# Second stage's edges: halves of the first batch in swapped parts, mask maxima one in three slots, last two turns interleaved

## The chip, the cores and the metric

The kernel runs on one core of a Trainium2 chip, alone on it. The metric is the device time of one execution in microseconds (us), the median of several runs. The core has five instruction streams: TensorE (PE, matrix products; its weight loads are listed as PEld), VectorE (DVE), ScalarE (ACT), GpSimd (POOL) and SyncE (SP, which here issues nearly all DMA transfers). Each stream runs its own instructions in order[...]. [...]

## The reference, cut to what matters

Input `x` is 128 graphs (batches) of 128 nodes with 128 features, `adj` an integer matrix 128 x 128 for each batch. Four graph layers follow one another, each as `x = x + layer(relu(layernorm(x)))`. The second of them is the one that this change touches:

```python
D = |x[:, :, None, :] - x[:, None, :, :]|          # (B, 128, 128, 128): all pairs of nodes
h = D @ W1.T + b1                                  # 64 features a pair
h = batchnorm(h; mean and variance over all pairs of all batches)
h = where(h >= 0, h, 0.01 * h)
s = h @ W2.T + b2                                  # one score a pair
s = where(A > 0, s, -9e15)                         # A: the adjacency
A = softmax(s)
y = (A @ x) @ Wg.T + bg
y = batchnorm(y; over all nodes of all batches)
y = where(y >= 0, y, 0.01 * y)
out = concat([x, y]) @ Wt.T + bt
```

The two batch norms take their statistics over everything, so nothing after the first can start before the last pair is in, and nothing after the second before the last `y` is there. They cut the kernel into three stages.

## The kernel before

**Stage one** (up to about 1455 us) computes the first graph layer and, for every batch, the products of `W1` with the pair differences. Symmetry halves the pairs: a batch needs the offsets 1 to 64 between two nodes, in two sets of 32, which stand on the two halves of the 128 partitions (64 features each). That gives `z`, 128 partitions x 4096 values a batch, kept as two **halves** of 128 x 2048 f32 (1 MB each). Of 124 batches they are written to HBM (`HP[b]`); those of the last four stay on chip. After that come the statistics of the first batch norm: `scale1`, `bias1`.

**Stage two** (to 2244 us) runs the 128 batches in **slots**, from -1 up to 140. The first four are those that stayed on chip; the others are read back from HBM by `fetch`. A ring of ten half-batch buffers holds them (`ahead_by` = 10): in slot `b`, SP issues the fetches of the halves `2 * b + 10` and `2 * b + 11` (L662), and each of them waits until its buffer in the ring, that of the half ten earlier, has been read for the last time. A slot does, for three batches at once:

- batch `b + 1`, preparation. The two halves go two different ways to the same function. The one called `z0` is scaled and shifted in place by ACT (L850) and made leaky by DVE, max of 0.01 z and z (L868). The one called `z1` is left as it is; ACT writes its scaled Relu to `zr` (L854).
- batch `b`, products. PE forms the scores in a bank `ps` (three of them), four matmuls for each part, 512 columns each: `w2z` with `z0`; then `w2l` with the raw `z1` (0.01 of scale and weight: the linear part) and `w2r` with `zr` (0.99 of the weight). A constant that the raw part lacks is put back by `add_k`, whose columns 4 to 7 belong to the half that went the second way and 0 to 3 to the other.
- batch `b - 1`, rearranging. DVE copies `ps` to `su` (L846), PE turns it with `pick` (L832, function `by_k`), DVE adds `add_k` and writes it to `sk` (L839, L841, function `to_sk`).

Four batches make a **turn**. A turn's function `chain` puts its steps into named places of coming slots with `at(slot, place, work)`; `slot` runs the places "am", "e", "p", "a", "l", "s" between its own instructions. So the order on every engine is written out by hand, and it is the order in which the engines run. In a turn, `to_rows` writes `sk` to HBM with a skewed address pattern and reads that turn's `x` (L902, L905); `from_rows` reads the scores back as `u` with rows and columns in place (L909); `normed` makes the layer norm on DVE (L244, L255), with the mask cap and `x + bt` on POOL (L914, L916); `folded` and `scores` add `u`, its transpose and the cap (L920, L924, L925); then maximum, exponential (L970, ACT), sums, weights, and products on PE with a copy to SBUF by ACT after each (L889, L894, L898, L948, L952). `stored` takes the statistics of `y` (L955). The turns' small PE results take three banks "sm" in rotation. Turn 31 is the last; the places of its steps are counted from `s0`, as are all.

In the slots 12 to 37 a side job, `brief`, works out whether a bound holds that lets stage three run without row maxima. It also looks for the largest value in the adjacency masks: `highest(g)`, one reduce over a mask of 128 x 512 bytes (L1045) for each of 32 groups, and `decided` at its end.

**Stage three** (430 us) needs the statistics of all `y` (L1116); its order comes from a planner and starts from the five groups that stayed on chip.

Of the kernel before, what the change touches and what calls it, by code (L numbers as in the profile page):

```python
# [13 lines left out]
AF = mybir.ActivationFunctionType  # L14
# [3 lines left out]
P = 128  # L18
G = 4
# [150 lines left out]
def tile_gnn_stack(ctx: ExitStack, tc: tile.TileContext, a: dict, out: bass.AP):  # L170
    nc = tc.nc
    NB = a["x"].shape[0]
    NG = NB // G
# [93 lines left out]
    def two_stages(general):  # L267
# [504 lines left out]
        with tc.tile_pool(name="c1", bufs=1, reuse_waits="tile") as c1, \  # L772
# [26 lines left out]

            sk = []  # L800
# [20 lines left out]
            def products(ps, parts, j0):  # L821
                for i, (w, v) in enumerate(parts):
                    for c in range(4):
                        w0 = 31 - 2 * (j0 // 4)
                        nc.tensor.matmul(ps[32 * c:32 * c + 32, :], w[:, w0:w0 + 32], v[:, 512 * c:512 * c + 512],  # L825
                                         start=j0 == 0, stop=w is w2r, skip_group_check=True)
# [8 lines left out]
            def to_sk(b):  # L835

                s, k, pk = sk[b // G % 2], b % G, scored.pop(b)[1]
                out_k = s[:, k, 1:].rearrange("p (a b) -> p b a", b=4)
                nc.vector.tensor_tensor(out_k, pk[:, :, 0:16], add_k.rearrange("p h j -> p (h j)")[:, None, :]  # L839
                                        .to_broadcast([P, 4, 16]), OP.add)  # L840
                nc.vector.tensor_scalar(s[:, k, 2 * KH:], s[:, k, 2 * KH:], 0.5, None, op0=OP.mult)  # L841

            def slot(b):
                if b - 1 in scored:
                    su = p1.tile([P, 4, P], F32, name="su")
                    nc.vector.tensor_copy(su.rearrange("p a b -> p (a b)"), scored[b - 1])  # L846
                    scored[b - 1] = su, sm("pk", "pk")
                if b + 1 < NB:
                    z0, z1 = fetched.pop(0), fetched.pop(0)
                    nc.scalar.activation(z0, z0, AF.Identity, bias=bias1, scale=scale1[:, 0:1])  # L850
                now(b, "am")
                if b + 1 < NB:
                    zr = p1.tile([P, NT // 2 * KC * P], F32, name="zr", bufs=3)
                    nc.scalar.activation(zr, z1, AF.Relu, bias=bias1, scale=scale1[:, 0:1])  # L854
                    prepared[b + 1] = z0, z1, zr
                now(b, "e")
                if b in prepared:
                    z0b, z1b, zrb = prepared.pop(b)
                    ps = psum.tile([P, 512], F32, tag="ps", bufs=banks["ps"], name="ps")
                    products(ps, [(w2z, z0b)], 0)  # L860
                    products(ps, [(w2l, z1b)], 4)
                if b - 1 in scored:
                    by_k(b - 1)
                if 0 <= b < NB:
                    products(ps, [(w2r, zrb)], 4)
                    scored[b] = ps
# [4 lines left out]
                if b - 1 in scored:  # L871
                    to_sk(b - 1)
                now(b, "l")
# [5 lines left out]
            def chain(turn):  # L879
# [5 lines left out]
                s0 = G * turn + 2 * G + 1 - 2 * final  # L885
# [14 lines left out]
                def to_rows():  # L900
                    to = rows[0, 0, 0:1]
                    nc.sync.dma_start(bass.AP(tensor=to.tensor, offset=to.offset,  # L902
                                              ap=[[ROW + 1, P], [P * ROW, G], [1, 1 + 2 * KH]]), own_sk)
                    t["x"] = p1.tile([P, G, P], F32, name="x", bufs=3)
# [33 lines left out]
                def weights():  # L938
                    nc.vector.tensor_tensor(t["e"], t["e"], t["sums"][:, :, None].to_broadcast([P, G, P]), OP.mult)
                    nc.vector.tensor_tensor(t["x1"], t["x1"], t["po"], OP.add)  # L940

                def product(name, left, right):
                    t[name] = sm(name)
                    four(t[name], left, right)
# [15 lines left out]
                at(G * turn + G + 1 - final, "s", to_rows)  # L960
                at(G * turn + G + 3 - 2 * final, "s", from_rows)
                at(s0, "e", normed)
                at(s0, "p", lambda: turned("pt", t["h"]))
                at(s0, "l", folded)
                at(s0 + 1, "am", lambda: copied("hT", "pt"))
                at(s0 + 1, "p", lambda: turned("put", t["u"]))
                at(s0 + 1, "l", scores)
                at(s0 + 2, "e", less_max)
                at(s0 + 2, "p", lambda: product("po", lambda k: t["hT"][:, k, :], lambda k: wtxT))
                at(s0 + 2, "a", lambda: nc.scalar.activation(t["e"], t["e"], AF.Exp))  # L970
                at(s0 + 2, "l", summed)
                at(s0 + 3, "e", weights)
                at(s0 + 3, "p", lambda: turned("pa", t["e"]))
                at(s0 + 3, "a", lambda: copied("aT", "pa"))
                at(s0 + 4, "p", lambda: product("py", lambda k: t["h"][:, k, :], lambda k: t["aT"][:, k, :]))
                at(s0 + 5, "am", lambda: copied("yT", "py"))
                at(s0 + 5, "p", last_product)
                at(s0 + 6, "am", biased)
                at(s0 + 7, "e", stored)
# [13 lines left out]
            def brief():  # L993
                t, end = {}, 3 * G
                searched = end + 9 + NG // 2
# [104 lines left out]
                for g in range(NG):  # L1100
                    at(end + 9 + g // 2, "l", lambda g=g: highest(g))
# [532 lines left out]
```

## Time and profile before

| | us |
|---|---|
| median of 3 runs | 2674.77 (2673.55 to 2675.49) |
| the profiled execution | 2676.09 |
| its span, first to last instruction | 2674.20 |
| DVE busy | 2469.6 (92% of the span) |
| PE busy | 2437.0 (91%) |
| ACT busy | 2380.3 (89%) |
| POOL busy | 1706.1 (64%) |
| first ACT pass of stage two | 1459.35 |
| first fetch of stage two issued | 1465.81 |
| last fetch of stage two issued | 2185.1 |
| aggregate of the statistics of `y` | 2244.33 |
| mean TensorE clock granted, share of full | 0.98 |

A line of the profile's order in time has the start in us, the duration in us, the engine, the line of the kernel (L...), the operation, the tiles written and read with their shapes, and how many; in brackets, how long the engine stood idle before it and what it waited for. A group line has the number of instructions, busy time in us, mean in ns, and the idle time before them. "issue" is time in which an engine waited for nothing that the profile shows. The DMA row of the page gives in tenths how full the 16 DMA engines are.

### The profile page before, as it was taken

What the parts mean: (1) busy time and instruction counts of PE and PEld (TensorE: products, weight loads), DVE (VectorE), ACT (ScalarE), POOL (GpSimd) and SP (SyncE); (2) the same over time, 40 slices, a digit from 0 to 9 for tenths busy, and PEclk for the clock granted to TensorE, in tenths of its full rate; (3) what the DMA queues carried; (4) which work ended last, traced back from release to release, by engine and by line L of the source; (5) the groups of instructions that cost most, each with busy time, mean ns of one, the idle gap of its engine ahead of it and who ended that gap; (6) DMA issues with size and microseconds to landing.
All of it is one profiled execution on the core that took longest, in us unless ns stands there. A gap on an engine that the chain in (4) does not pass through costs nothing.

```text
span 2674.2 us, 41925 instructions
## 1 busy us (share of the span) xinstructions
PE 2437.0 (91%) x14521; PEld 1162.1 (43%) x14521; DVE 2469.6 (92%) x4738; ACT 2380.3 (89%) x2821; POOL 1706.1 (64%) x1628
## 2 busy tenths in 40 slices
PE   6999999999999999999997988888888886999997
PEld 3333333333333333333332443444444445777776
DVE  5999999999999999999998789988888886899997
ACT  5999999999999999999998877788778874999997
POOL 6999999999999999999985000010101123666663
PEclk8999999999999999999998999999999998999999
DMA  3555555555555555555542999999999992021211
GB/s 101 201 206 209 212 212 211 212 213 205 209 205 209 205 210 204 217 204 216 205 197 93 409 409 384 392 409 410 411 410 411 410 373 81 21 68 56 64 37 34
DMA packets 185426, 611.43 MB, mean 229 GB/s; under 512 B 31987, under 2 KB 99702, under 8 KB 121718
## 3 DMA queue, kind: packets, MB, share of 16 engines
q1 hardware_dynamic: 184768, 608.50, 59.1%
q8 instruction: 118, 1.93, 0.3%
q14 instruction: 102, 0.84, 0.1%
q10 hardware_dynamic: 438, 0.17, 0.0%
HBM read 312.58 MB, written 296.03 MB: 228 GB/s over the span
## 4 chain that ended last, share of the span: by engine, by line
PE 37%; ACT 24%; DVE 15%; DMA 12%; POOL 7%; issue 4%; SPq 0%; POOLq 0%; DVEq 0%; ACTq 0%
PE hp L338 16%; ACT d L376 9%; ACT z L352 7%; DMA z<-hp 4%; PE hp L341 4%; DMA rows<-sk 4%; PE ps L825 4%; POOL d L328 4%; DMA u<-rows 3%; DVE z L868 3%; ACT o L473 2%; PE pk L832 2%; ACT hn L473 2%; PE xp L414 1%; DVE e L1502 1%
## 5 line engine op out<-in xcount | busy, mean ns | idle before, releaser
L328 POOL TENSOR_TENSOR d<-xe 128x2048 f32<-128x2048 f32 x256 | 1073.8, 4205 | 36.4 <-PE hp L338 34.5
L338 PE MATMUL hp<-d,w1T 128*64 128x512 f32 x4096 | 994.1, 601 | 57.6 <-ACT z L352 54.5
L376 ACT ACTIVATE d<-d 128x2048 f32<-128x2048 f32 x384 | 733.8, 1924 | 19.8 <-POOL d L328 19.5
L328 DVE TENSOR_TENSOR d<-xe,xp 128x2048 f32<-128x2048 f32 x256 | 583.6, 2280 | 7.0 <-POOL xe L423 4.0
L352 ACT COPY z<-hp 128x1024 f32<-128x1024 f32 x512 | 519.1, 1015 | 9.7 <-PE hp L338 4.5
L338 PEld LDWEIGHTS hp<-d,w1T 128*64 128x64 f32 x4096 | 276.9, 136 | 559.5 <-issue 455.3
L916 POOL TENSOR_TENSOR x<-x,bt 128x512 f32<-128x512 f32 x32 | 48.8, 1525 | 665.7 <-DMA x<-x 494.1
L366 DVE BATCH_NORM_STATS2 st<-z 128x6 f32<-128x512 f32 x512 | 354.7, 693 | 6.2 <-ACT z L352 6.1
L367 DVE BATCH_NORM_STATS2 st<-z 128x6 f32<-128x512 f32 (+1 forms) x512 | 336.4, 657 | 0.0
L868 DVE SCALAR_TENSOR_TENSOR z<-z 128x2048 f32<-128x2048 f32 x128 | 299.5, 2340 | 5.5 <-ACT z L850 5.3
L850 ACT ACTIVATE z<-z,bias,scale 128x2048 f32<-128x2048 f32 x128 | 267.5, 2090 | 8.9 <-DVE bias L762 7.7
L854 ACT ACTIVATE zr<-z,bias,scale 128x2048 f32<-128x2048 f32 x128 | 267.7, 2092 | 0.5 <-DMA z<-hp 0.5
L341 PE MATMUL hp<-both_t,xw 128*64 128x512 f32 x1024 | 265.2, 592 | 0.0
L825 PE MATMUL ps<-z,w2z 128*32 128x512 f32 x1024 | 140.9, 622 | 61.2 <-DVE z L868 60.5
L832 PEld LDWEIGHTS pk<-pick,su 128*128 128x128 f32 x1024 | 126.8, 195 | 147.8 <-DVE su L846 112.9
L832 PE MATMUL pk<-pick,su 128*128 128x16 f32 x1024 | 139.4, 268 | 34.6 <-DVE su L846 33.8
L825 PE MATMUL ps<-zr,w2r 128*32 128x512 f32 x1024 | 142.5, 629 | 0.0
L341 PEld LDWEIGHTS hp<-both_t,xw 128*64 128x64 f32 x1024 | 77.6, 137 | 142.2 <-issue 142.2
L825 PE MATMUL ps<-z,w2l 128*32 128x512 f32 x1024 | 138.4, 610 | 0.0
L1525 PE MATMUL pv<-wr,e 128*128 128x128 f32 x1024 | 134.0, 278 | 2.1 <-ACT wr L1450 1.1
L1525 PEld LDWEIGHTS pv<-wr,e 128*128 128x128 f32 x1024 | 124.1, 192 | 8.4 <-ACT wr L1450 1.8
L1409 ACT ACTIVATE h<-x,nb,rs 128x128 f32<-128x128 f32 x256 | 106.0, 491 | 20.1 <-POOL nb L1404 18.4
(241 smaller groups left out, 3808.3 us busy)
## 6 DMA issues: line engine op xcount, KB each, us to landing
hp<-z SPq DMA_DIRECT2D x248, 1024.0 KB, 4.0
z<-hp SPq DMA_DIRECT2D x248, 1024.0 KB, 13.7
x<-x SPq DMA_DIRECT2D x118, 256.0 KB, 4.8
u<-rows SPq DMA_DIRECT2D x32, 384.0 KB, 11.4
x<-in_x_dram SPq DMA_DIRECT2D x32, 256.0 KB, 5.6
adj<-in_adj_dram SPq DMA_DIRECT2D x32, 256.0 KB, 5.9
out_dram<-x SPq DMA_DIRECT2D x32, 256.0 KB, 2.4
z<-y SPq DMA_DIRECT2D x27, 256.0 KB, 11.8
```

Of the source, the lines that this page charges most:

```text
L328: eng.tensor_tensor(d, ahead, x[:, None, None, :].to_broadcast([P, 2, KC, P]), OP.max if t == BY_MAX else OP.subtract)
L338: nc.tensor.matmul(hp[64 * hh:64 * hh + 64, c:c + 512], w1T2 if by_max else w1T, d[:, hh, c:c + 512], start=True, stop=not by_max, skip_gr ...
L341: nc.tensor.matmul(hp[64 * hh:64 * hh + 64, c:c + 512], XW[i // NT // 2][:, i // NT % 2, :], both_t.rearrange("p h k i -> p h (k i)")[:, h ...
L352: nc.scalar.copy(half_of(b, t), linear.pop(i))
L366: nc.vector.bn_stats(st[:, 2 * t, :], hs[:, 0:512])
L367: nc.vector.bn_stats(st[:, 2 * t + 1, :], hs[:, 512:1024 - P * last])
L376: nc.scalar.activation(diffs[i], diffs[i], AF.Abs)
L825: nc.tensor.matmul(ps[32 * c:32 * c + 32, :], w[:, w0:w0 + 32], v[:, 512 * c:512 * c + 512], start=j0 == 0, stop=w is w2r, skip_group_chec ...
L832: nc.tensor.matmul(pk[:, kk, 0:16], su[:, kk, :], pick.rearrange("p h j -> p (h j)"), start=True, stop=True)
L850: nc.scalar.activation(z0, z0, AF.Identity, bias=bias1, scale=scale1[:, 0:1])
L854: nc.scalar.activation(zr, z1, AF.Relu, bias=bias1, scale=scale1[:, 0:1])
L868: nc.vector.scalar_tensor_tensor(z0, z0, 0.01, z0, op0=OP.mult, op1=OP.max)
```

## The change

Three parts.

- First batch: `z0` and `z1` change places in slot -1, and ACT makes the Relu before the linear pass. In slot 0, PE takes the raw part first, then the Relu part, then `w2z`. As the columns of the scores change with the places, a second constant tile, `add_0` (sixteen columns of the scratch tile `selfb`), holds `add_k` with its two parts swapped.
- Mask maxima: `highest(g)` goes to slot `end + 9 + 3 * g` with `end` = 12: 32 reduces in the slots 21, 24, ... 114; before, two in each of the slots 21 to 36. `decided` moves to slot 118.
- Last two turns: turns 30 and 31 get plans of their own, and a new place "k", just behind `to_sk`. The read of `x` becomes a function of its own, `again`. Turn 30 starts up to three slots earlier (its read-back `u` at slot 126, not 127; norm 126, not 129), and its value product goes to a bank "ps". Turn 31 asks for its `x` at slot 125, before its rows; its rows go out in slot 128 as before. The steps of both turns alternate. `joined` is split off `weights`. Turn 29 moves one ACT step by part of a slot.

```diff
+            add_0 = selfb[:, G - 1, P - 16:].rearrange("p (h j) -> p h j", h=2)
+            nc.vector.tensor_copy(add_0[:, :, 4:8], add_k[:, :, 0:4])
+            nc.vector.tensor_copy(add_0[:, :, 0:4], add_k[:, :, 4:8])
...
-            def products(ps, parts, j0):
-                for i, (w, v) in enumerate(parts):
-                    for c in range(4):
-                        w0 = 31 - 2 * (j0 // 4)
-                        nc.tensor.matmul(ps[32 * c:32 * c + 32, :], w[:, w0:w0 + 32], v[:, 512 * c:512 * c + 512],
-                                         start=j0 == 0, stop=w is w2r, skip_group_check=True)
+            def products(ps, w, v, j0, start=False, stop=False):
+                for c in range(4):
+                    w0 = 31 - 2 * (j0 // 4)
+                    nc.tensor.matmul(ps[32 * c:32 * c + 32, :], w[:, w0:w0 + 32], v[:, 512 * c:512 * c + 512],
+                                     start=start, stop=stop, skip_group_check=True)
...
-                nc.vector.tensor_tensor(out_k, pk[:, :, 0:16], add_k.rearrange("p h j -> p (h j)")[:, None, :]
+                nc.vector.tensor_tensor(out_k, pk[:, :, 0:16], (add_k if b else add_0).rearrange("p h j -> p (h j)")[:, None, :]
...
+                linear = lambda z: nc.scalar.activation(z, z, AF.Identity, bias=bias1, scale=scale1[:, 0:1])
+                first = b + 1 == 0
                 if b + 1 < NB:
                     z0, z1 = fetched.pop(0), fetched.pop(0)
-                    nc.scalar.activation(z0, z0, AF.Identity, bias=bias1, scale=scale1[:, 0:1])
+                    if first:
+                        z0, z1 = z1, z0
+                    else:
+                        linear(z0)
                 now(b, "am")
                 if b + 1 < NB:
                     zr = p1.tile([P, NT // 2 * KC * P], F32, name="zr", bufs=3)
                     nc.scalar.activation(zr, z1, AF.Relu, bias=bias1, scale=scale1[:, 0:1])
+                    if first:
+                        linear(z0)
...
-                    products(ps, [(w2z, z0b)], 0)
-                    products(ps, [(w2l, z1b)], 4)
+                    if b:
+                        products(ps, w2z, z0b, 0, start=True)
+                    products(ps, w2l, z1b, 4 * (b > 0), start=b == 0)
                 if b - 1 in scored:
                     by_k(b - 1)
                 if 0 <= b < NB:
-                    products(ps, [(w2r, zrb)], 4)
+                    products(ps, w2r, zrb, 4 * (b > 0), stop=b > 0)
+                    if b == 0:
+                        products(ps, w2z, z0b, 4, stop=True)
...
                 if b - 1 in scored:
                     to_sk(b - 1)
+                now(b, "k")
                 now(b, "l")
...
-                s0 = G * turn + 2 * G + 1 - 2 * final
+                s0 = G * turn + 2 * G + 1
...
+                if last < 2:
+                    at(s1, "s", to_rows)
+                    at(s1, "s", again)
+                    at(s1 + 2 - last, "s", from_rows)
+                else:
+                    at(s1 - 4, "s", again)
+                    at(s1 - 1, "s", to_rows)
+                    at(s1, "s", from_rows)
...
+                elif last == 1:
+                    plan = ((-3, "k", normed), (-2, "p", lambda: turned("pt", t["h"])), (-2, "k", folded),
+                            (-2, "l", lambda: turned("put", t["u"])), (-1, "am", lambda: copied("hT", "pt")),
+                            (-1, "k", scores), (0, "e", less_max), (0, "p", lambda: values("ps")), (0, "a", exps),
+                            (0, "l", summed), (1, "e", weights), (1, "p", lambda: turned("pa", t["e"])),
+                            (1, "a", lambda: copied("aT", "pa")), (2, "p", mixed), (2, "a", lambda: copied("yT", "py")),
+                            (3, "e", joined), (3, "p", last_product), (4, "am", biased), (5, "e", stored))
+                else:
+                    plan = ((-4, "k", normed), (-3, "p", lambda: turned("pt", t["h"])),
+                            (-3, "a", lambda: copied("hT", "pt")), (-3, "k", folded),
+                            (-3, "l", lambda: turned("put", t["u"])), (-2, "e", scores),
+                            (-2, "p", lambda: values("ps")), (-2, "l", less_max), (-1, "am", exps), (-1, "k", summed),
+                            (-1, "k", weights), (0, "e", joined), (0, "p", lambda: turned("pa", t["e"])),
+                            (0, "a", lambda: copied("aT", "pa")), (1, "p", mixed), (1, "a", lambda: copied("yT", "py")),
+                            (2, "p", last_product), (2, "a", biased), (2, "l", stored))
...
-                searched = end + 9 + NG // 2
+                searched = end + 9 + 3 * NG
...
-                    at(end + 9 + g // 2, "l", lambda g=g: highest(g))
+                    at(end + 9 + 3 * g, "l", lambda g=g: highest(g))
```

`last` is 1 for turn 30, 2 for turn 31 and 0 for all others, whose plan is the one from before; `s1` is `4 * turn + 5`.

## The prediction

> **What bounds the kernel now.** I read the page's slices first, to find where the DMA queues set the pace; then the engines' busy time in chosen stretches of the second stage; then the order in time at its two edges.
>
> ```profile
> DMA  3555555555555555555542999999999992021211
> GB/s 101 201 206 209 212 212 211 212 213 205 209 205 209 205 210 204 217 204 216 205 197 93 409 409 384 392 409 410 411 410 411 410 373 81 21 68 56 64 37 34
> ```
>
> A slice is 66.9 us. From slice 22 to slice 32, counted from 0 (about 1460 to 2200 us) the DMA engines are full at 410 GB/s: this is the second stage, which reads 248 halves of 1 MB back. Two slices in it show only 384 and 392. The stretches below (columns: width, busy us of PE, PE loads, DVE, ACT, POOL, then granted clock, DMA share, GB/s) place that dip.
>
> ```profile
> 1594.00:1697.00 103.00, 86.82 (x633) 41.43 (x633) 96.83 (x157) 75.36 (x52) 9.48 (x9) 0.95 1.01 384
> 1744.00:2172.00 428.00, 376.61 (x2882) 181.37 (x2881) 367.46 (x566) 342.97 (x237) 56.83 (x36) 0.98 1.03 410
> 2180.00:2200.00 20.00, 17.13 (x134) 8.17 (x126) 16.52 (x23) 15.18 (x12) 3.50 (x2) 1.00 0.94 372
> 2200.00:2220.00 20.00, 17.97 (x137) 9.71 (x138) 17.80 (x36) 10.19 (x9) 2.70 (x3) 1.00 0.19 49
> 2220.00:2245.00 25.00, 15.27 (x68) 11.22 (x67) 14.87 (x29) 7.23 (x12) 1.27 (x1) 0.80 0.33 100
> ```
>
> In the first row DVE is busy 96.83 of 103 us (94%) and DMA gets 384; in the second DVE has 86% and DMA 410. So the long stretch is bound by DMA, the short one by DVE, and the reason is one group: `L1045`, the mask maxima, 32 of 0.674 us, all between 1584.2 and 1685.2 us. After 2200 the DMA is nearly idle and no engine is full: latency.
>
> ```profile
> 1459.35 2.10 ACT L850 ACTIVATE z<-z,bias,scale 128x2048 f32<-128x2048 f32 x1 [7.71 <-DVE bias L762]
> 1461.47 2.29 DVE L868 SCALAR_TENSOR_TENSOR z<-z 128x2048 f32<-128x2048 f32 x1 [0.52 <-ACT z L850]
> 1463.82 1.93 PE L825 MATMUL ps<-z,w2z 128*32 128x512 f32 x8 [3.21 <-DVE z L868]
> 1465.81 2.06 SPq L662 DMA_DIRECT2D z<-hp  x2
> ```
>
> At the first edge ACT, DVE and PE follow one another, and only when PE has read the first half does its buffer come free and the first transfer of the stage start, at 1465.81.
>
> ```profile
> 2218.87 0.15 DVE L841 TENSOR_SCALAR sk<-sk 128x1 f32<-128x1 f32 x1
> 2219.05 0.36 SPq L902 DMA_DIRECT2D rows<-sk  x1
> 2222.26 0.36 SPq L909 DMA_DIRECT2D u<-rows  x1
> 2224.20 0.69 DVE L924 TENSOR_TENSOR e<-u,pt 128x512 f32<-128x512 f32 x1 [3.36 <-PE pt L894]
> 2229.35 0.40 DVE L920 TENSOR_TENSOR u<-u 128x256 f32<-128x256 f32 x1
> 2243.60 0.69 DVE L955 BATCH_NORM_STATS2 ST<-y 128x6 f32<-128x512 f32 x1 [2.51 <-ACT y L952]
> 2244.33 1.02 DVE L1116 BATCH_NORM_AGGREGATE mv<-ST 128x2 f32<-128x192 f32 x1
> ```
>
> At the last edge the final turn (31) writes its scores at 2219.05 and reads them back as `u`, issued at 2222.26; by one-microsecond stretches the DMA moves that until 2225.6. Yet `u` is folded only at 2229.35, since DVE is busy with turn 30 (the line at 2224.20), and the stage ends at 2244.33. Stage three follows it unchanged, 430 us.
>
> **The change, part by part.**
>
> *Mask maxima.* 32 reduces stay, from two in each of 16 slots to one in every third of 94. In the packed stretch four turns (u issues of 1594.06 to 1697.39) took 103.3 us. From 1743.98 to 2172.13, 18 turns took 428.15, 23.79 each; four are 95.2. That is 8.2 us lost; the next two turns took 46.6 instead of 47.6, so 1.0 was regained: 7.2. By bytes: 103 x (1 - 384/410) = 6.5. I take 7.0. What does the spread cost? Per turn it adds 4/3 x 0.64 = 0.85 us (two back to back take 1.27) to a DVE busy 367.46/18 = 20.4 of 23.79. It hides under the transfers while the compute loop stays under 23.79 a turn. How near is that loop? Slots 122 to 126, whose data had landed by about 2199, ran at 5.7 us each, 22.8 a turn. The packed stretch added 8 x 0.63 = 5.1 us to 22.8 and gave 25.8, so 0.6 of what is added lies on the loop: 22.8 + 0.6 x 0.85 = 23.3, under 23.79 by 0.5. Thin, so I charge 0.5 in all: **-6.5**, ends -7.2 (nothing) and -3 (a turn half over the line, 24 turns x 0.17).
>
> [...]
>
> *First batch.* Its halves change roles: half 0 now needs only Relu on ACT and two products on PE (`w2l` on the raw half, `w2r` on the Relu); half 1 gets the linear ACT pass, the DVE pass and `w2z` last. `w2l` is ready at 1459.48. PE's order puts one of its four matmuls, then the two small ones of L779 and L792 (0.58 and 0.56), then three: four took 1.70 us at half clock (1463.82 to 1465.52), so half 0 is read by about 1462.3, Relu ending at 1461.43. The first fetch starts at 1462.6, not 1465.81. Half 1: ACT to 1463.4, DVE to 1465.8, `w2z` to 1467.5: the second fetch at 1467.8, against 1467.56 now; the third and fourth (1470.05, 1470.94) 0 to 0.5 earlier. A half takes 1.05 MB/410 = 2.56 us. Now the queues run without a gap from about 1466.6. Then one transfer is over by 1466.0 and they stand until 1468.6: 2.56 saved, 2.0 given back, **-0.5**. [...] PE, busy from 1459.5, would be fast for `w2z`, the second fetch would go at 1467.0 and this part be -1.4. The rows had 0.50 until 1468 for work begun at 1463.82, over 4 us; and PE now pauses 1.8 us before `w2z`. I keep half clock. The two copies into `add_0` (0.16 each) fall into DVE's waits for PE at 1454.5 and for ACT at 1461: free. Without that cover, 0.3.
>
> *Last two turns.* Turn 30 moves up two to three slots. Its norm (1.54 us DVE) goes into slot 126 behind `to_sk`, ahead of the scores of turn 29, where DVE waits 1.5 us now (2209.78 to 2211.29): hidden. Its fold (0.42) meets a 0.3 us wait at 2215.1: +0.1. Its eight transposes (2 x 0.63 on PE) now stand ahead of the last `pick` products (2216.92), which have about 0.4 to spare: the last `to_sk` slips from 2218.57 to 2218.9. Its read-back on SP goes a slot earlier with only POOL and DVE work behind it that has slack; both `x` loads (256 KB) go at slot 125, when the DMA share is 0.4 to 0.7, and turn 31's no longer shares the queue with its rows. POOL's `cap` and `x + bt` move up into idle time; the products of `hT` take a `ps` bank, free by then.
>
> Then, on the old clock: rows at 2219.4, `u` issued 3.2 later and landed 3.3 later, at 2225.9. Meanwhile DVE has turn 30's scores, maximum and difference (2.75), turn 31's norm (1.54), turn 30's sums and weights (1.55): from 2219.4 to 2225.3, with 0.5 of waits; so it stands ready. Fold 2226.4; transposes 0.63 and the hop, 2227.2; scores 1.4 and maximum 1.4, 2230.1; exp 0.63 under turn 30's join and turn 29's statistics (1.4), 2231.4; sums and weights 1.55, 2233.0; transposes 0.63, copy 0.6, product 1.16, copy 0.6, product 1.12, bias 0.69, statistics 0.69 with seven hops of 0.1 to 0.2: 2239.5. Against 2244.3: -4.8. PE pauses here 2 us and more, and in the profile at 2230 to 2232 its clock was 0.5, four transposes 1.09 instead of 0.63: if all of the chain's PE work runs so, +2.3. I charge 0.3: **-4.5**, ends -6 and -2.
>
> *Sum:* -6.5 - 0.5 - 4.5 = -11.5. The profiled execution took 2676.09 (span 2674.20 and 1.89 around it), so 2664.6 of that kind. It lies 1.3 above the median of the runs, 2674.77; on that, **2663.3 us**.
>
> **Rivals.**
>
> *Compute paces the rest.* If the spread reduces lie on a loop as long as the transfers, half of the first gain goes: 24 turns x 0.15 = 3.6, giving 2667. For it: 22.8 against 23.79. Against: 410 GB/s throughout.
>
> *No gain from the reduces.* The missing bytes would have to be regained later anyway; two turns at 23.3 regained 1.0 of 8.2, so little speaks for it. Then -5.0: 2669.8.
>
> *Upper ends everywhere:* -7.2 - 1.4 - 6: 2660.2, and a little further if the earlier data also shortens slots 122 to 128.
>
> *Slower.* Each spread reduce, at the end of its slot, holds up the next `su` copy on DVE, so `pick` and `w2r` on PE, so the next copy: one loop through two engines, in which it would cost its full 0.64. Then 32 x 0.64 = 20.5, less 7.0 + 0.5 + 4.5: +8.5, 2683. It decides from 12.0/32 = 0.38 us a reduce. Against it: the packed stretch cost only 7.2/32 = 0.23 each.
>
> **How the numbers follow.** The likeliest case 0.58 (2663.3, own range 2659 to 2667); compute paces 0.18 (2667); no gain from the reduces 0.11 (2669.8); upper ends 0.08 (2660); slower 0.05 (2683). About 0.2%, 5.3 us, is what a measurement of this kernel can tell from no change: faster means under 2669.4. The first two, the fourth and nearly a third of the third: 0.87 faster, 0.08 same, 0.05 slower. The range leaves out the slower case and little else: 2657 to 2670.
>
> **What would show it.** Maxima: the stretch 1594 to 1697 at 408 to 412 GB/s, turns of 23.8 there, DVE near 89% to 2150; wrong if GB/s sinks under 405 over 1744 to 2100. First edge: the first fetch near 1462.6 and a hole in the queues of some 2.5 us behind it; wrong if the hole is not there. Last edge: the fold of turn 31 within 1 us of `u` landing, and 13 to 14 us from there to the aggregate (18.7 now). The whole is wrong if the spread reduces slow the loop, or if the last `to_sk` slips by more than a microsecond against the last landing of z.

## The result, and the profile after

The changed kernel takes **2664.7 us** (median of 6 runs, 2663.6 to 2668.8); the kernel before 2674.95 (6 runs, the three of the table above among them). The ratio is 0.9963 with a 95% interval of 0.995 to 0.9975, that is 9.9 us less (6.7 to 13.4). Predicted were 2663.3 us and a range of 2657 to 2670. The profiled execution took 2664.61, its span 2662.8.

The page's slices of the changed kernel, DMA fullness in tenths and GB/s:

```profile
DMA  3555555555555555555542999999999992021211
GB/s 102 201 206 210 208 211 210 212 212 208 211 209 210 208 212 207 209 206 210 206 194 95 402 410 410 411 411 409 410 410 411 407 372 85 21 69 57 64 37 34
```

The two slices with 384 and 392 GB/s are gone: between its first slice and its last the second stage now moves 407 to 411 throughout. The same stretches as in the prediction (columns: width, busy us of PE, PE loads, DVE, ACT, POOL, then granted clock, DMA share, GB/s):

```profile
1594.00:1697.00 103.00, 88.74 (x694) 42.59 (x687) 92.45 (x144) 82.48 (x57) 11.26 (x9) 1.00 1.02 410
1744.00:2172.00 428.00, 372.30 (x2853) 179.17 (x2854) 375.16 (x588) 338.24 (x235) 42.45 (x36) 0.99 1.03 410
2180.00:2200.00 20.00, 16.95 (x126) 7.79 (x128) 19.50 (x29) 14.32 (x11) 3.48 (x3) 0.91 0.73 250
2200.00:2220.00 20.00, 16.38 (x120) 9.65 (x113) 17.92 (x37) 6.66 (x9) 1.89 (x2) 0.99 0.18 46
2220.00:2245.00 25.00, 14.72 (x73) 11.85 (x72) 14.32 (x29) 9.16 (x14) 8.86 (x15) 0.66 0.35 122
```

In the first row DVE has 92.45 us instead of 96.83; in the second it has 7.7 us more than before and DMA still gets 410. New are the granted clocks of 0.91 and 0.66 in the third and fifth rows: PE now runs at half clock for part of the last slots and for more than half of the last chain.

The first edge in order of time:

```profile
1459.24 2.09 ACT L863 ACTIVATE zr<-z,bias,scale 128x2048 f32<-128x2048 f32 x1 [7.71 <-DVE bias L762]
1459.43 1.91 PE L829 MATMUL ps<-z,w2l 128*32 128x512 f32 x2 [2.04 <-DVE w2l L790]
1463.35 4.50 DVE L882 SCALAR_TENSOR_TENSOR z<-z 128x2048 f32<-128x2048 f32 x2 [0.65 <-ACT z L852]
1464.22 2.92 SPq L662 DMA_DIRECT2D z<-hp  x2
1465.70 1.07 PE L829 MATMUL ps<-z,w2z 128*32 128x512 f32 x8
```

The first fetch goes at 1464.22, not at the 1462.6 of the prediction. The trace has two records for each of these matmuls, so the second line is one matmul of `w2l`, and it takes 1.91 us, as long as the four of `w2z` (x8) took at half clock before. But `w2z` now takes 1.07 us and not 1.93: PE is at full clock (granted 1.00 from 1465.39, where before it was 0.50 until 1468.95). The last edge:

```profile
2213.35 0.15 DVE L845 TENSOR_SCALAR sk<-sk 128x1 f32<-128x1 f32 x1
2213.53 0.37 SPq L917 DMA_DIRECT2D rows<-sk  x1
2216.17 0.36 SPq L926 DMA_DIRECT2D u<-rows  x1
2219.53 0.42 DVE L937 TENSOR_TENSOR u<-u 128x256 f32<-128x256 f32 x1 [0.17 <-DMA u<-rows]
2222.01 0.69 DVE L941 TENSOR_TENSOR e<-u,pt 128x512 f32<-128x512 f32 x1 [2.06 <-PE pt L909]
2234.11 0.69 DVE L974 BATCH_NORM_STATS2 ST<-y 128x6 f32<-128x512 f32 x1 [5.24 <-ACT y L971]
2234.84 1.02 DVE L1155 BATCH_NORM_AGGREGATE mv<-ST 128x2 f32<-128x192 f32 x1
```

DVE now waits for `u` (0.17 us at the fold) where before `u` waited for DVE: the fold is 6.2 us behind the last `to_sk`, before 10.5. From the fold to the aggregate, though, it takes 15.3 us; before it took 15.0.

Both spans, cut at the same marks (us). B is the start of the bias of the first norm (L762); U the issue of `u` at 1594.06 before and 1592.04 after, where the packed stretch begins; F the end of the last line of `z` fetches on SP's queue (2184.48 + 2.10 before, 2176.19 + 2.08 after); T the last `to_sk`.

| stretch | before | after | difference | predicted |
|---|---|---|---|---|
| start to B | 1459.09 | 1458.99 | -0.1 | 0 |
| B to U, first edge | 134.97 | 133.05 | -1.9 | -0.5 |
| U to F, transfers | 592.52 | 586.23 | -6.3 | -6.5 |
| F to T, last slots | 32.29 | 35.08 | +2.8 | +0.3 |
| T to fold of turn 31 | 10.48 | 6.18 | -4.3 | -3.3 |
| fold to aggregate | 14.98 | 15.31 | +0.3 | -1.6 |
| aggregate to end, stage three | 429.87 | 427.96 | -1.9 | 0 |

The predicted values of the two rows of the last chain are the prediction's own times (fold at 2226.4, 7.2 behind the last `to_sk`; aggregate at 2239.5, 13.1 behind the fold, and 0.3 for the clock). The sum is -11.4, near the predicted -11.5, but four rows are off by 1.4 to 2.5 us each. The experiments are about these rows. Each ran beside the kernel before on the same chip.

### The profile page after: what moved, and what is told of

Read it like the earlier page. It is cut to its first block, busy times and chain, and to the rows that moved or that the text cites. A ratio compares the mean times of both kernels' runs of the same rounds, so it can differ in the third digit from the quotient of the medians.

```text
span 2662.8 us, 41921 instructions
## 1 busy us (share of the span) xinstructions
PE 2428.4 (91%) x14521; PEld 1155.7 (43%) x14521; DVE 2468.4 (93%) x4740; ACT 2379.2 (89%) x2821; POOL 1689.3 (63%) x1628
## 3 DMA queue, kind: packets, MB, share of 16 engines
q8 instruction: 118, 1.93, 0.3%
## 4 chain that ended last, share of the span: by engine, by line
PE 37%; ACT 22%; DMA 15%; DVE 12%; POOL 7%; issue 6%; SPq 0%; POOLq 0%; ACTq 0%; DVEq 0%
PE hp L338 16%; ACT z L352 7%; ACT d L376 7%; DMA rows<-sk 6%; DMA z<-hp 5%; DMA u<-rows 4%; PE hp L341 4%; POOL d L328 4%; PE ps L829 4%; DVE z L882 2%; ACT o L473 2%; ACT hn L473 2%; PE pk L836 1%; DVE e L1541 1%; PE xp L414 1%
## 5 line engine op out<-in xcount | busy, mean ns | idle before, releaser
L366 DVE BATCH_NORM_STATS2 st<-z 128x6 f32<-128x512 f32 x512 | 348.2, 680 | 6.1 <-ACT z L352 6.0
L367 DVE BATCH_NORM_STATS2 st<-z 128x6 f32<-128x512 f32 (+1 forms) x512 | 329.7, 644 | 0.0
L882 DVE SCALAR_TENSOR_TENSOR z<-z 128x2048 f32<-128x2048 f32 x128 | 293.1, 2291 | 6.4 <-ACT z L852 6.4
## 6 DMA issues: line engine op xcount, KB each, us to landing
u<-rows SPq DMA_DIRECT2D x32, 384.0 KB, 11.5
```

The lines of the kernel that those rows point to most:

```text
L366: nc.vector.bn_stats(st[:, 2 * t, :], hs[:, 0:512])
L367: nc.vector.bn_stats(st[:, 2 * t + 1, :], hs[:, 512:1024 - P * last])
L882: nc.vector.scalar_tensor_tensor(z0, z0, 0.01, z0, op0=OP.mult, op1=OP.max)
```

## The experiments

**The three parts alone.** The kernel before with one part each.

```diff
-                searched = end + 9 + NG // 2
+                searched = end + 9 + 3 * NG
...
-                    at(end + 9 + g // 2, "l", lambda g=g: highest(g))
+                    at(end + 9 + 3 * g, "l", lambda g=g: highest(g))
```

> The kernel before with only the mask maxima spread (one in every third slot). Theory of the prediction: the two-in-a-slot reduces made DVE the bound for 100 us, the spread ones hide under the transfers: -6.5 us, 2668.5 (the trace of the changed kernel says -6.1 net), the stretch 1594 to 1697 back at 410 GB/s. Rival, no gain from the reduces since the ring makes up for the lost bytes later: 2674 to 2675, with the stretch after 1700 above 410 GB/s in the kernel before. Rival, each spread reduce costs its full 0.64 us on the loop of DVE and PE: plus 14, 2689.

Measured: 2669.1 (11 runs), ratio 0.998 (0.9971 to 0.9989): -5.3 us, between -7.8 and -2.9. In the profile, U to F is 585.88 (before 592.52): -6.6, and the stretch is full:

```profile
1594.00:1697.00 103.00, 91.80 (x682) 43.73 (x674) 89.51 (x144) 80.06 (x56) 11.12 (x9) 0.95 1.02 410
```

Both rivals fall: nothing is given back later, and no reduce costs its full time. But F to T is 36.07 here, 3.8 more than before, without any of the new plans. So the loss in the last slots does not come from the plans alone.

```diff
+                    if first:
+                        z0, z1 = z1, z0
...
+                    if first:
+                        linear(z0)
...
+                    if b == 0:
+                        products(ps, w2z, z0b, 4, stop=True)
```

> The kernel before with only the first batch's halves in swapped parts. The prediction's own value: -0.5 us, with PE at half clock for the w2z products and a hole of 2.5 us in the queues behind the first fetch. What the trace of the changed kernel says: -2.0 us (PE, at work from 1459.4, is at full clock for w2z; 0.85 MB more have been moved 10 us into the stage, 2.07 us at 410 GB/s). Rival, the ring evens out whatever is gained at the start: 0.

Measured: 2674.63 (14 runs), ratio 1.0001 (0.9993 to 1.0009): no difference. B to U is 134.44, -0.5, the size of the prediction, with `w2z` at half clock:

```profile
1462.63 5.26 SPq L662 DMA_DIRECT2D z<-hp  x3
1464.11 1.94 PE L829 MATMUL ps<-z,w2z 128*32 128x512 f32 x8
```

The order of the instructions is the changed kernel's, and PE's first product starts 6.27 us before `w2z` in both (1457.84 to 1464.11, and 1459.43 to 1465.70); only the clock differs. The -0.5 is then lost in the packed stretch, which takes 103.98 us here, 103.33 before and 100.65 in the next experiment: with two reduces in a slot this stretch alone differs by 3 us between runs. With the reduces spread it is 95.3 to 95.9 in the changed kernel, with the maxima alone and in the two pairs of parts below.

```diff
+                elif last == 1:
+                    plan = ((-3, "k", normed), (-2, "p", lambda: turned("pt", t["h"])), (-2, "k", folded),
...
+                else:
+                    plan = ((-4, "k", normed), (-3, "p", lambda: turned("pt", t["h"])),
...
```

> The kernel before with only the new plans of the last two turns. The prediction's value: -4.5 us, of it the shorter chain from u's landing to the aggregate (18.7 to 13.5) and 0.3 lost by the last to_sk. The changed kernel's trace says: the chain 18.7 to 15.3 and 2.8 us lost in the slots 123 to 128 (PE at half clock after a pause, GpSimd's x + bt of turn 30 beside DVE), so -1.3 in stage two, and -1.9 in stage three that no step explains: between -1.3 and -3.2. If the loss in the slots 123 to 128 comes from the earlier data of the other two parts and not from the plans, -4 and more.

Measured: 2672.51 (13 runs), ratio 0.9989 (0.9981 to 0.9997): -2.9 us, between -5.1 and -0.8. T to the fold is 6.04 (before 10.48), fold to aggregate 15.12, and F to T 33.70: the plans bring 4.4, shorten nothing behind the fold, and cost 1.4 in the last slots. Stage three takes 429.69: the -1.9 of the changed kernel's profile is not theirs. Over all fourteen profiles of this study stage three takes 427.5 to 430.1, whatever the second stage is.

**Two parts at a time.** The changed kernel without the new plans, and the changed kernel without the first batch's swap (the diffs above, taken out).

> The changed kernel with the last two turns as before: the first batch's swap and the spread maxima only. If the first batch is worth -2 once the packed stretch no longer sets the pace, the median lies 2 under the spread maxima alone: -6.8 against before, and the changed kernel is faster than this one by 3 to 4, the tail's own worth beside the spread. If the first batch is worth -0.5 or nothing in the mean (the granted clock at its w2z differs from run to run: full in the changed kernel's profile, half when tried alone), -5.3 to -5.5 against before. In the slots 123 to 128 the same 2.6 to 3.8 us are lost as with the spread maxima alone, since the cause (GpSimd's x + bt of turn 29 starting just ahead of DVE's weights) does not come from the plans.

> The changed kernel with the first batch as before: spread maxima and the new plans of the last two turns. If the first batch is worth -2 in the changed kernel, this is 2 slower than it: -7.9 against before; if -0.5, -9.4. Against the spread maxima alone it shows the tail's worth: the profiles say -4.1 at the aggregate (238.95 to 234.84, 2000 left off).

Measured: 2666.22 (8 runs), ratio 0.9973 (0.9963 to 0.9984), and 2666.07 (7 runs), ratio 0.9971 (0.996 to 0.9982): -7.2 and -7.8 against the -9.9 of all three. That puts each part at 2 to 3 us in the company of the others, but the intervals, of about 3 us to each side, are too wide to show it. B to U is 133.59 with the swap (`w2z` 1.62 us) and 134.82 without. The expectation of a loss of 2.6 to 3.8 us in the last slots held for the second (F to T 37.14) and missed for the first (33.42), where DVE's weights came just behind GpSimd's `x + bt`, beside its next instruction, the mask cap of 0.62 us, and took 1.07 us. The meeting (shown below) is a matter of tenths of a microsecond.

**The cost of the spread reduces.** The changed kernel with 31 of the 32 reduces left out, so that the largest value is that of one group's masks only:

```diff
-                    nc.vector.tensor_reduce(t["tops"][:, g:g + 1], M8[g].rearrange("p a b -> p (a b)"), AX.X, OP.max)
+                    if g == 0:
+                        nc.vector.tensor_reduce(t["tops"][:, g:g + 1], M8[g].rearrange("p a b -> p (a b)"), AX.X, OP.max)
+                        for n in range(1, NG):
+                            nc.vector.tensor_copy(t["tops"][:, n:n + 1], t["tops"][:, 0:1])
```

> The changed kernel with 31 of the 32 mask reduces left out (each of the other 31 columns is a copy of the first by DVE in slot 21, so the flag rests on one group's mask only; 31 copies of one column there). Theory: the spread reduces lie under the transfers, so leaving them out gains 0 to 0.5 us against the changed kernel (2664.7), DVE loses 20 us of busy time and the end does not move. Rival, the loop of DVE and PE paces the stage too: -3.6 or more. Between them: the small copies cost 31 x 0.06 in slot 21, about 2 us of DVE once, which the ring of ten halves covers.

Measured: 2664.64 (5 runs), ratio 0.9961 (0.9948 to 0.9974), the changed kernel's own. U to F is 586.47 without the reduces and 586.23 with them. They cost nothing.

**Other spacings.** One reduce in each of 32 slots, and four in each of eight.

```diff
-                    at(end + 9 + 3 * g, "l", lambda g=g: highest(g))
+                    at(end + 9 + g, "l", lambda g=g: highest(g))
```

> The changed kernel with the mask maxima one in every slot, 21 to 52 (not one in every third). A turn then has 2.56 us of reduces on DVE. By DVE's busy time 20.4 + 2.6 = 23.0 a turn, under the 23.79 of the transfers: 0. By the prediction's step that 0.6 of what is added lies on a loop of 22.8: 24.3 a turn, 8 turns half a microsecond too long: +4, 2669, with 400 to 405 GB/s in that stretch.

Measured: 2664.23 (7 runs), ratio 0.9965 (0.9953 to 0.9977); U to F 585.96. No cost.

```profile
1594.00:1697.00 103.00, 88.51 (x692) 42.36 (x684) 96.56 (x158) 81.33 (x57) 9.71 (x10) 1.00 1.02 410
```

This row has DVE as busy as the row of before had it (96.83), and 410 GB/s where that had 384. The busy share did not tell the two apart; the turns do, below.

```diff
-                    at(end + 9 + 3 * g, "l", lambda g=g: highest(g))
+                    at(end + 9 + g // 4, "l", lambda g=g: highest(g))
```

> The changed kernel with the mask maxima four in each of the slots 21 to 28. A turn then has 10.2 us of reduces. By DVE's busy time: 30.6 a turn against 23.8, two turns: +13.6, less what the ring of ten halves covers and the stretch behind regains. By 0.6 of what is added on a loop of 22.8: 28.9 a turn, +10.3, less 1 regained. If a reduce just costs the 0.23 that it cost two in a slot: +7.

Measured: 2675.3 (22 runs), ratio 1.0009 (1.0001 to 1.0016), slower than before by 2.4 us (0.3 to 4.3).

```profile
1580.00:1640.00 60.00, 43.16 (x316) 21.23 (x316) 57.16 (x94) 38.15 (x27) 6.06 (x4) 0.94 0.96 361
```

Two turns take 30.08 and 28.48 us (u issues at 1591.89, 1621.97 and 1650.45), the next 23.07; U to F is 595.89, 9.7 more than in the changed kernel. In total that is the value of the second theory, 10.3 less 1. The turns say more than the total. DVE's busy time in single turns, from one issue of `u` to the next (us; turns at the ends of the bunched stretch, which hold fewer reduces, are left out):

| turn from | reduces in it | length | DVE busy | rest |
|---|---|---|---|---|
| before, 1594.06 | 7 | 26.12 | 24.70 | 1.42 |
| before, 1620.18 | 9 | 26.30 | 24.88 | 1.42 |
| before, 1646.48 | 8 | 25.71 | 24.29 | 1.42 |
| four a slot, 1591.89 | 15 | 30.08 | 28.66 | 1.42 |
| one a slot, four turns from 1592.64 | 4 each | 23.47 to 24.26 | 21.89 to 22.67 | 1.58 or 1.59 |

In the four turns where DVE sets the pace (the first four rows), a turn is its busy time and 1.42 us; all that is added to DVE counts. Some 19.5 us of these turns are other work (24.6 less 5.1 for eight reduces, 22.1 less 2.7 for four), so DVE's loop without reduces is, by estimate, about 21 us, not 22.8. With one reduce a slot it is 22.1 and 1.42, about 23.6, just under the 23.79 of the transfers: no cost. With two it is about 26, with four 30 and more. The prediction's step, 0.6 of what is added on top of 22.8, met the 25.8 that it was taken from and came near with four a slot (28.9 a turn), but for one a slot it foretold 24.3, where the turns took 23.8.

**The last slots.** In the prediction's terms the last `to_sk` was to slip 0.3 us. In the order of time of the changed kernel GpSimd adds `bt` to the `x` of turn 29 as soon as that has landed, while DVE has the weights of turn 28:

```profile
2188.01 1.27 POOL L933 TENSOR_TENSOR x<-x,bt 128x512 f32<-128x512 f32 x1 [21.26 <-DMA x<-x]
2188.08 1.74 DVE L956 TENSOR_TENSOR e<-e,sums 128x512 f32<-128x512 f32 x1
2192.77 1.93 PE L829 MATMUL ps<-z,w2z 128*32 128x512 f32 x8 [2.24 <-DVE z L882]
```

In the kernel before, the same two, and the same products of slot 125:

```profile
2196.36 0.68 DVE L939 TENSOR_TENSOR e<-e,sums 128x512 f32<-128x512 f32 x1
2196.41 1.76 POOL L916 TENSOR_TENSOR x<-x,bt 128x512 f32<-128x512 f32 x1 [19.31 <-DMA x<-x]
2200.47 1.06 PE L825 MATMUL ps<-z,w2z 128*32 128x512 f32 x8 [1.84 <-DVE z L868]
```

There DVE came first by 0.05 us and took 0.68; GpSimd was stretched to 1.76. Here GpSimd came first by 0.07, and DVE took 1.74. Behind that PE stood 2.24 us instead of 1.84, and its products then ran at half clock (the granted clock is 0.50 from 2192.43 to 2195.85). The experiment asks for that `x` one slot earlier:

```diff
-                    at(s1, "s", again)
+                    at(s1 - (turn == NG - 3), "s", again)
```

> The changed kernel with one load moved: x of turn 29 is asked for one slot earlier (120, not 121), so that GpSimd's x + bt (L933) of that turn is over some 6 us before DVE's weights (L956) at the place where they met. Theory: weights takes 0.68 us and not 1.74, PE's pause before w2z of slot 125 falls from 2.24 to about 1.2, the clock stays at 1.00 there, the last to_sk comes 2 to 2.7 us sooner against the last fetch, and the time falls by 2 to 2.7 against the changed kernel. Rival: the new plans themselves (transposes ahead of the pick products, extra DVE work) hold the last slots up; then w2z stays late and nothing moves, 0. Against both: x + bt meets another DVE operation at its new place; the transfers still set the pace there, so that costs nothing.

```profile
2181.42 1.27 POOL L933 TENSOR_TENSOR x<-x,bt 128x512 f32<-128x512 f32 x1 [15.69 <-DMA x<-x]
2188.13 0.67 DVE L956 TENSOR_TENSOR e<-e,sums 128x512 f32<-128x512 f32 x1
2191.75 1.06 PE L829 MATMUL ps<-z,w2z 128*32 128x512 f32 x8 [1.35 <-DVE z L882]
```

All three steps of the theory are there: weights 0.67, a pause of 1.35, full clock. F to T is 33.61 instead of 35.08: -1.5, less than the 2 to 2.7 expected. `x + bt` did meet another DVE instruction at its new place (L948 at 2181.89 takes 1.35 us and not 0.69), under the transfers. The median, 2664.68 (5 runs), ratio 0.9968 (0.9955 to 0.998), does not show the 1.5: by the times alone it stays open. The profiles of all kernels together show it (us; the half clock is the one that began behind PE's pause before slot 125's products):

| plans, kernels | weights of turn 28 | half clock | F to T |
|---|---|---|---|
| old: before; first batch alone | 0.68; 0.67 | none | 32.29; 32.32 |
| old: without the plans | 1.07 | none | 33.42 |
| old: maxima alone | 1.75 | 6.8 | 36.07 |
| new: plans alone; earlier load; all together (below) | 0.67 | none | 33.61 to 33.71 |
| new: four a slot; one a slot | 1.07; 0.96 | not read | 33.64; 33.99 |
| new: changed kernel; without reduces; the next two below | 1.74 or 1.75 | 3.4 | 35.08 to 35.27 |
| new: without the swap | 1.66 | 6.8 | 37.14 |

The plans alone cost 1.3 to 1.4. With the full meeting it is 1.4 to 1.7 more where the half clock behind it lasts 3.4 us, and 3.4 to 3.8 more where it lasts 6.8. What the plans' own 1.4 is made of was not separated; in it is a second such meeting, `x + bt` of turn 31, moved up by the plans, beside L948, which takes 1.38 us instead of 0.69 with the earlier load, in the changed kernel and with the plans alone.

**PE's order in the last chain.** `L941` above waits 2.06 us for `pt`: the transposes of `u` stand on PE behind those of turn 30's weights and of turn 31's norm.

```diff
-                    plan = ((-4, "k", normed), (-3, "p", lambda: turned("pt", t["h"])),
+                    plan = ((-4, "k", normed), (-3, "e", lambda: turned("pt", t["h"])),
```

> The changed kernel with the four transposes of turn 31's norm moved ahead of turn 29's last product and turn 30's weights on PE (place e of slot 130, not p). In the changed kernel they stand between turn 30's weights and turn 31's put, which waits 0.86 us for them at half clock. Theory: put, scores and everything behind come 0.9 us sooner, the aggregate too: -0.9 and u's landing to aggregate 15.3 to 14.4. Rival: what PE gains it loses elsewhere, the chain being paced by the clock that drops in PE's pauses: 0.

Measured: 2663.62 (5 runs), ratio 0.9963 (0.995 to 0.9976). The wait of L941 fell from 2.06 to 0.83 us, and fold to aggregate is 14.99 instead of 15.31. Neither can be put down to the move. With PE's order unchanged the wait is 0.77 in the kernels with one and with four reduces a slot and 0.81 with the earlier load, where the transposes ran at full clock; in the changed kernel they took 0.85 and 1.06 instead of 0.63. And over the seven profiles with the new plans and that order fold to aggregate is 14.52 to 16.18. The earlier load, 14.76, has 6.5 us at half clock in it, the longest 9.4. What came sooner at the scores here went again at the end of the chain, where the last two products of turn 31 ran at half clock (2.08 us for `py` and for `pz`, after a pause of 2.93). So the rival fits, with 7.6 us of this chain at half clock, and the move's own worth is not shown.

**PE kept at work in the last chain.** 36 transposes of the identity, whose result nobody reads, in PE's waits:

```diff
+                def warm(n):
+                    if "w" not in t:
+                        t["w"] = sm("warm", "ps")
+                    for _ in range(n):
+                        for k in range(G):
+                            nc.tensor.transpose(t["w"][:, k, :], ident, ident)
...
+                            (-4, "a", lambda: warm(2)), (-1, "a", lambda: warm(5)), (0, "a", lambda: warm(1)),
+                            (1, "a", lambda: warm(1)))
```

> The changed kernel with idle PE work added in the last turn's waits: 36 transposes of the identity into a spare bank (8 behind turn 30's value product, 20 behind its last product, 4 and 4 around turn 31's mixed product), read by nobody. Theory: what the chain from u's landing to the aggregate has too much (15.3 for the predicted 13.5) is the granted clock, which falls to 0.5 in PE's pauses (0.67 over 2220 to 2240): with PE kept at work the four transposes take 0.63 instead of 0.85 to 1.06, the last product 1.13 instead of 2.08, and from the fold of turn 31 to the aggregate it is 13.2 to 13.8 instead of 15.3: -1.5 to -2.1. Rival: the clock doesn't follow PE's own work here, or the added transposes stand in front of real ones: 0 to +1.

```profile
2219.56 0.43 DVE L937 TENSOR_TENSOR u<-u 128x256 f32<-128x256 f32 x1 [0.56 <-DMA u<-rows]
2223.26 2.35 PE L984 MATMUL warm<-ident 128*128 128x128 f32 x20
2226.57 0.63 PE L909 MATMUL pt<-ident,e 128*128 128x128 f32 x4 [0.96 <-DVE e L956]
2229.81 1.12 PE L967 MATMUL pz<-yT,wgT 128*128 128x512 f32 x2 [0.29 <-ACT yT L913]
2232.42 1.02 DVE L1164 BATCH_NORM_AGGREGATE mv<-ST 128x2 f32<-128x192 f32 x1
```

Fold to aggregate is 12.86, without half clock in it: 2.45 less than in the changed kernel, a little more than expected, and 1.7 to 3.3 less than in the seven profiles just named. `pz` takes 1.12 instead of 2.08. The median is 2663.13 (6 runs), ratio 0.9962 (0.9948 to 0.9975): 1.6 under the changed kernel's, too little for the intervals and not measured side by side.

**All of these together**, with 32 more such transposes behind the last product (`(2, "l", lambda: warm(8))`):

> The changed kernel with the earlier load of x for turn 29, the transposes of turn 31's norm moved ahead, and the idle PE work of the warm kernel, 32 more such transposes behind the last product. If the parts add: -1.5 in the slots 123 to 128, -1.5 to -2.1 in the chain, and up to -0.5 at the start of stage three, where PE's first products run at half clock now: 2660.5 to 2662 against 2664.7. If the earlier load only moves the meeting of GpSimd and DVE elsewhere, 2663.

Measured: 2660.96 (5 runs, 2659.97 to 2662.91), ratio 0.9955 (0.9941 to 0.9968), that is 12.0 us less than before on that chip (8.6 to 15.8). Beside it the warm kernel had 2663.13 and the kernel with one reduce a slot 2664.23. It has the lowest median of all; against the changed kernel the ratios' intervals overlap. Its fold to aggregate is 12.86 again, and stage three takes 427.54 with the granted clock at 1.00 from 2235 to 2240, where the changed kernel has 0.50. That is the shortest of the fourteen, but only 0.4 under one that had no such transposes; so what they bring to stage three is not shown. Its profiled execution was the slowest of the five: U to F takes 589.17 there, 3 us more than in the other kernels without bunched reduces (585.4 to 586.5). What caused that was not tried.

## Why the prediction was right

*Mask maxima, -6.5: right, but not by its loop.* U to F gained 6.3, with the part alone 6.6. The reading behind it held: 384 GB/s was a stretch paced by DVE, and with the reduces spread the same stretch moved 410, as the long one did before and after. The step that failed is "22.8 a turn" with "0.6 of what is added lies on the loop". The turns show a loop of DVE's busy time and 1.42 us, about 21 without reduces, on which all that is added counts; at two a slot both sums give the same, since the 0.6 was fitted there. So the charge of 0.5 for the spread was too much, and leaving the reduces out gained nothing. The rival "compute paces the rest" is out: even one reduce in every slot cost nothing, though that is only about 0.2 us a turn under the transfers. "Slower" is out too.

*First batch, -0.5: right in the order of its steps, its clock was a matter of the run.* The first step that failed is "I keep half clock". B to U over all profiles, by what `w2z` took:

| | `w2z`, us | B to U, us |
|---|---|---|
| halves as before (four profiles) | 1.93 or 1.94 | 134.64 to 135.09 |
| swapped, half clock or nearly (part alone; one reduce a slot) | 1.94; 1.74 | 134.44; 134.29 |
| swapped, between (without the plans; without reduces) | 1.62; 1.23 | 133.59; 133.48 |
| swapped, full or nearly (the changed kernel and five more) | 1.07 to 1.14 | 132.77 to 133.26 |

At half clock the swap is worth about -0.4 against the mean of the first row, near the -0.5 of the sum but no more than that row's own spread; at full clock it is worth -1.9. That PE would be fast for `w2z`, and the part then -1.4, was an estimate of the author's; against it stood one trace, with half clock until 1468. The runs show both: with the same order and the same 6.27 or 6.28 us from PE's first product to `w2z`, `w2z` took anything from 1.07 to 1.94. In seven of these ten profiles the moment of the full clock was read: 5.5 (earlier load) to 8.7 us (part alone) after PE's first product. What set that moment was not shown. The prediction took the one trace and chose a side; it should have split the part between -0.5 and -1.9. Its first fetch at 1462.6 was wrong too (1464.22): the first of the four `w2l` matmuls was taken at a quarter of 1.70 us. In the traces the four matmuls of a part start within 0.03 us of one another and run side by side, so one alone takes as long as four: 1.91 us in the changed kernel, against 1.93 for four at half clock before. The hole behind the first fetch, whose absence the prediction named as its sign of being wrong, was not there in the changed kernel; at half clock a smaller one was, as 303 and 242 GB/s in the two stretches of 2 us from 1464 of the part alone.

*Last two turns, -4.5: right in its main step, wrong in two sizes.* T to the fold: DVE does stand ready when `u` lands, and that brought 4.3, 1.0 more than worked out, of which 0.6 is SP's: `u` is issued 2.64 us behind the rows and not 3.2, with no load of `x` between them. "I charge 0.3" for PE's pauses was the first wrong size: kept at full clock the chain from the fold takes 12.86, close to the 13.1 of the prediction's working (2226.4 to 2239.5); as it is it takes 15.31, and 14.5 to 16.2 over the seven profiles. The price is 2.45 here, the +2.3 that the prediction named and did not take. "The last `to_sk` slips from 2218.57 to 2218.9" was the second: F to T grew by 2.8. Of it about 1.4 goes with the meeting of GpSimd and DVE and the half clock behind it, shown by the earlier load and by the table of all profiles, and about 1.4 is the plans' own. The prediction counted the plans' instructions on DVE, PE and SP and gave GpSimd "idle time"; it did not ask which DVE instruction runs at the same moment. In the two profiles shown the later of the two pays: DVE 0.68 and GpSimd 1.76 us where DVE came first, GpSimd 1.27 and DVE 1.74 where GpSimd did. By an estimate from these times, a second that did nothing until the first was over would take 1.90 and 1.88; measured is 0.14 less. Why the two hold each other up was not shown. By the prediction's own words a slip of more than a microsecond would make the whole wrong. It was 2.8, and the total still held, for the first edge brought 1.4 more than charged, the fold came 1.0 sooner, and stage three, by no step of the change, came out 1.9 shorter in that execution.

*The sum, -11.5.* It stands at -9.9 in the runs and -11.4 in the profiled pair. That pair flatters the change: without stage three's scatter it has -9.5. So the sum was too large by about 2, well inside its range, and it came out right partly by luck, because errors of both signs met.

## What to carry to other kernels

Side work on a busy engine is free as long as the engine's own loop stays under what paces the stage: the same 32 reduces cost nothing at one a slot, 6.3 us at two and 9.7 at four, against one in three slots. DVE's busy share (94% in the first two cases) did not tell which; its microseconds a turn, with 1.42 for its waits, set beside the 23.79 of the transfers, did. Where a stage is a chain of waits, as the last chain is here, look up the granted clock before PE's steps are priced: the last product took 2.08 us behind PE's pauses in the changed kernel (one of 2.53, clock 0.50 from 2229.98) and 1.12 with them filled; filling them with work that nobody reads was worth 2.45 us of 15.3 in the profiles, and in the times too little to be told from scatter. When an instruction of GpSimd starts as soon as a load lands, look up which DVE instruction runs at that time: here a shift of about 0.1 us decided whether GpSimd took 1.76 us and not 1.27, or DVE 1.74 and not 0.68.

## What the runs showed of the hardware that was not expected

- In six profiles a pause of PE of 2.23 or 2.24 us before the products of slot 125 was followed by half clock at once or within a slot; in the six others where PE's order was read there, the pause was 1.34 to 1.88 us, and no half clock followed.
- After PE had gone to work at the first edge, the full clock came 5.97 us later in the changed kernel (1465.39; first product 1459.43) and 8.73 us later with the part alone (1466.57; 1457.84), with the same instructions. Behind the pause above, the half clock lasted 3.4 us in four profiles and 6.8 us in two. In the profiles of before and of the changed kernel, the changes of the granted clock lie 3.41 us or a multiple of it apart (2192.43 and 2195.85; 1455.15 and 1465.39).
- DVE's weights (0.68 us by themselves) and GpSimd's `x + bt` (1.27), when they met: in the kernel before, with DVE first by 0.05 us, `x + bt` took 1.76; in the changed kernel, with GpSimd first by 0.07, the weights took 1.74.
- One matmul of `w2l`, alone, took 1.91 us at half clock in the changed kernel, as long as four of `w2z` side by side in the kernel before (1.93).
